# Moving the scores' matmuls next to the values' product in a pipelined macaron kernel on Trainium2

## The chip, the cores and the metric

The kernel runs on one core of one Trainium2 chip. The time is what the device takes for one execution, in microseconds (us); lower is better. The kernel before took 2442.0 us (median of three runs, 2439.76 to 2442.17).

## The reference, cut to what matters

Four sequences of 4096 rows of 512 numbers pass through half of a feed-forward layer, an attention in which each query sees 13 neighbouring keys, and the other half of the feed-forward layer:

```python
x = x + 0.5 * ffn(layernorm(x), ffn_w, ffn_b)     # both operands rounded to a 6-bit grid in blocks of 32
x = x + attention(layernorm(x), qkv_w, qkv_b, rpb, proj_w, proj_b)
x = x + 0.5 * ffn(layernorm(x), ffn_w, ffn_b)
# attention: 16 heads of 32, query i sees keys clip(i - 6, 0, L - 13) .. + 12
attn = softmax(einsum('bhld,bhlkd->bhlk', q, k[nbr]) + rpb[:, bidx])
out  = einsum('bhlk,bhlkd->bhld', attn, v[nbr]) @ proj_w.T + proj_b
```

## The kernel before, in words

**Tiles and items.** The 16384 rows are 128 tiles of 128 rows. Four tiles make a group of 512 rows. The attention of one group for four of the sixteen heads is an item, so there are 128 items as well, and the loop takes one tile and one item a step. An item's queries are cut into blocks of 30 (16 to 18 blocks an item), and a block of queries meets 42 keys.

**Numbers.** Every float32 operand of a large product is held as a high and a low half in 16-bit floats, so one 128 x 512 product is 12 matmuls (`product`, L146 to L154: high by low, low by high, high by high, over four slices of 128).

**Slots.** Nothing schedules this program but the order in which it is written. Each stage is a Python generator (`first_half`, `values`, `project_qk`, `softmax`, `attend`, `project_out`, `second_half`, `quantised_norms`); `begin` (L162) puts it into a slot, `run_slot` (L165) runs the stages of a slot in the order of their rank, and `yield n, rank` sends the rest of a stage n slots on. Seven slots are a step (`STEP`, L559), and L562 says in which slot each stage of item or tile 0 begins. What an engine is handed in this order it does in this order: a waiting instruction holds up all that is behind it on its engine, and on SP's queue of transfers.

**One step on the PE (TensorE).** In the order of the slots: the second feed-forward's product `pmf` and then the item's scores `ps` (slot 0 of the step), the output projection `pmo` (slot 2), the queries' projection `pmqk` and then the values' product `pv` of the item two steps ahead (slot 3), the keys' projection `pmqk` (slot 4), the first feed-forward's product `pmf` (slot 5), the values' projection `pmv` (slot 6). The six products are each 12 matmuls over the whole 128 x 128 array. The scores are 8 small matmuls a block, 32 rows by 32 columns (`num_active_cols=32`, L433), and the values' product is 4 small matmuls a block, 126 rows by 32 columns (L503). Each matmul has a weight load of its own, so with 17 blocks a step is 144 instructions of the six products, 272 of the scores and 136 of the values' product.

**Buffers.** The six products share three PSUM buffers (`ps_m`, L93), so each product needs the result of the third product before it to be read: `pmv` takes the buffer of the queries' `pmqk`, which VectorE (DVE) empties last, in `put_low(0)` (L371 to L375, called at L384). Scores and values' product have one PSUM buffer each.

**An item's way.** `project_qk` (L349): two products, then `put_high` on ScalarE (ACT) and `put_low` on DVE for queries and keys. `softmax` (L417): scores on PE, bias and sum on DVE (L458, L461), the maximum on DVE (L465), its subtraction on GpSimd (POOL, L467), the exponential on ACT (L469), total and reciprocal on DVE (L472 to L474), the scaling on POOL (L476), the high half twice on ACT (L480, L481) and the low half on POOL (L483) into the one tile `p`, and a transposing transfer to `pT` on SP's queue (L485). `attend` (L488): the values' product from `pT` and the stack `vs` of shifted values (loaded from DRAM at L409), then its two halves into `ring` on ACT and DVE (L530, L536).

**Others that share the queues.** `quantised_norms` (L220) makes two tiles' operand `xT` for `pmf` with DVE, POOL and ACT, and sends it through SP (L205), as `first_half` does for `x2`, the operand of `pmv` and `pmqk`.

Of the kernel before, what the change touches and what calls it, by code (L numbers as in the profile page):

```python
# [64 lines left out]
def macaron_kernel(  # L65
# [63 lines left out]
    def bc(t, n):  # L129

        return t.unsqueeze(2).to_broadcast([t.shape[0], t.shape[1], n])
# [14 lines left out]
    def product(pm, lhs, rhs):  # L146

        n = 0
        for a, b in ((0, 1), (1, 0), (0, 0)):
            for c in range(KC):  # L150
                nc.tensor.matmul(  # L151
                    pm, lhs(a, c), rhs(b, c), start=(n == 0), stop=(n == 3 * KC - 1)
                )
                n += 1  # L154
# [7 lines left out]
    def begin(slot, stage, rank=5):  # L162
        slots.setdefault(slot, []).append((rank, stage))
# [155 lines left out]
    def span(j):  # L319

        q0 = min(j * QN, length - QN)
        return q0, min(max(q0 - NS, 0), length - KN)

    def kind(j):
        return 1 if j == 0 else 2 if j == n_blocks - 1 else 0

    def late(j):

        return QR - QN if j == n_blocks - 1 else 0
# [14 lines left out]
    def item_of(m):  # L344

        g, c = divmod(m, KC)
        return g // NG, g % NG, c

    def project_qk(m):  # L349

        b, g, c = item_of(m)
        xg = x2[b * NG + g]
        t = qkp.tile([P, 2, 2, KN + GT], F16, tag="qk", name=f"qk{m}")
        qk[m] = t
        pms = []

        def project(s):
            pm = ps_m.tile([P, GT], F32, tag="mm", name=f"pmqk{s}_{m}")
            pms.append(pm)
            o = (QO, KO)[s] + c * P  # L360
            product(
                pm,
                lambda a, kc: wt[:, a, kc, o : o + P],
                lambda a, kc: xg[:, a, kc].rearrange("p i q -> p (i q)"),
            )

        def put_high(s):
            bias = qk_b[:, s, c : c + 1]
            nc.scalar.activation(t[:, s, 0, KN:], pms[s], AF.Identity, bias=bias)  # L369

        def put_low(s):  # L371
            bias = qk_b[:, s, c : c + 1]
            nc.vector.scalar_tensor_tensor(  # L373
                t[:, s, 1, KN:], pms[s], bias, t[:, s, 0, KN:], ALU.add, ALU.subtract
            )  # L375

        project(0)
        yield 1, 5
        project(1)
        put_high(0)  # L380
        if g > 0:
            nc.scalar.copy(t[:, :, :, :KN], halo[:, c])  # L382
        yield 1, 6
        put_low(0)  # L384
        put_high(1)
        if c == KC - 1:
            del x2[b * NG + g]
        yield 1, 0
        put_low(1)
        yield 2, 8  # L390
        if g + 1 < NG:
            nc.scalar.copy(halo[:, c], t[:, :, :, GT:])
# [24 lines left out]
    def softmax(m):  # L417

        b, g, c = item_of(m)
        j0, j1 = group_blocks[g]  # L420
        n = j1 - j0
        t = qk.pop(m)


        ps = ps_s.tile([P, 3, 2, 256], F32, tag="s", name=f"ps{m}")
        for i in range(n):
            q0, k0 = (KN + at - g * GT for at in span(j0 + i))
            q0 -= late(j0 + i)
            u, w = divmod(i, PSB)
            for part, sides in ((0, 2), (1, 1)):  # L430
                for h in range(4):
                    rows = slice(h * D, (h + 1) * D)
                    nc.tensor.matmul(  # L433
                        ps[rows, u, :sides, w * KN : (w + 1) * KN],
                        t[rows, 0, part, q0 : q0 + QR], t[rows, 1, :sides, k0 : k0 + KN],
                        start=part == 0, stop=part == 1,
                    )

        def pieces(i, e):

            while i < e:
                u, w = divmod(i, PSB)
                whole = max((e - i) // PSB, 1) if w == 0 else 1
                f = min(e, (u + whole) * PSB)
                yield slice(u, u + whole), slice(w, w + (f - i) // whole)
                i = f

        yield 1, 9
        sf = sfp.tile([P, MAXB, KN], F32, tag="sf", name=f"sf{m}")
        s4 = sf.rearrange("p (u w) k -> p u w k", w=PSB)  # L450
        p4 = ps[:, :, :, : PSB * KN].rearrange("p u a (w k) -> p a u w k", k=KN)
        first = 1 if kind(j0) == 1 else 0
        last = n - (1 if kind(j1 - 1) == 2 else 0)
        for i, e in ((0, first), (first, last), (last, n)):
            for u, w in pieces(i, e):
                o = s4[:, u, w, :]
                bias = table[:, kind(j0 + i), c, :].unsqueeze(1).unsqueeze(1).to_broadcast(o.shape)
                nc.vector.tensor_tensor(o, p4[:, 0, u, w, :], bias, ALU.add)  # L458
        for u, w in pieces(0, n):
            o = s4[:, u, w, :]  # L460
            nc.vector.tensor_tensor(o, o, p4[:, 1, u, w, :], ALU.add)  # L461
        yield 1, 2
        s = sf[:, :n, :]
        top = sm.tile([P, MAXB], F32, tag="top", name=f"top{m}")
        nc.vector.tensor_reduce(top[:, :n], s, AX.X, ALU.max)  # L465
        yield 1, 4
        nc.gpsimd.tensor_tensor(s, s, bc(top[:, :n], KN), ALU.subtract)  # L467
        yield 1, 9
        nc.scalar.activation(s, s, AF.Exp, scale=alpha)  # L469
        yield 1, 4  # L470
        total = sm.tile([P, MAXB], F32, tag="total", name=f"total{m}")
        nc.vector.tensor_reduce(total[:, :n], s, AX.X, ALU.add)  # L472
        nc.vector.reciprocal(total[:, :n], total[:, :n])  # L473
        nc.vector.tensor_tensor(total[:, :n], total[:, :n], p_scale[:, :n], ALU.mult)  # L474
        yield 1, 4
        nc.gpsimd.tensor_tensor(s, s, bc(total[:, :n], KN), ALU.mult)  # L476
        yield 2, 8
        p = p_tile
        ph = p[:, :n, :KN]
        nc.scalar.copy(ph, s)  # L480
        nc.scalar.copy(p[:, :n, 2 * KN : KV], ph)  # L481
        yield 2, 4
        nc.gpsimd.tensor_tensor(p[:, :n, KN : 2 * KN], s, ph, ALU.subtract)  # L483
        pT = ptp.tile([P, MAXB, P], F16, tag="pT", name=f"pT{m}")
        nc.sync.dma_start_transpose(out=pT[:, :n, :], in_=p[:, :n, :].rearrange("p n k -> p (n k)"))  # L485
        probs[m] = pT
# [71 lines left out]
    EARLY = 3  # L558
    STEP = 7  # L559

    F1, V, QK, SC, PV, OUT, F2 = 5, 2 * STEP + 6, 5 * STEP + 3, 6 * STEP, 8 * STEP + 3, 13 * STEP + 2, 12

    def add_bias(t, b):
        nc.gpsimd.tensor_tensor(xs[t], xs[t], b, ALU.add)  # L564
# [27 lines left out]
    for t in range(NT):  # L592
        k = t * STEP
# [16 lines left out]
    for m in range(n_items):  # L610
        k = m * STEP
        begin(k + QK, project_qk(m))
        begin(k + SC, softmax(m), 6)
        begin(k + PV, attend(m), 6)
    for n in range(n_batch * NG):
        k = n * GROUP * STEP
# [295 lines left out]
```

## Time and profile before

| what | value |
|---|---|
| runs (us) | 2442.17, 2442.00, 2439.76; median 2442.0 |
| the profiled execution | 2436.42 us, its span 2434.6 us |
| mean granted TensorE clock | 0.992 |
| step (from one item's scores to the next, 1201.9 to 1220.7 us as an example) | 18.80 us: PE 18.07 busy, DVE 16.42, POOL 15.89, ACT 10.41 |
| six products | 380 ns a matmul as the profile models it; a new one starts every 216 ns |
| scores `ps` L433 | 17536 matmuls, 164.0 us and 162.0 us busy in two shapes |
| values' product `pv` L503 | 8768 matmuls, 90.3 us busy |

The profile is one execution. An engine's busy time overlaps itself on PE (a matmul's end is modelled), so starts are compared with starts here. "Idle before" is the time that an engine stood still ahead of an instruction, with what ended it; "issue" means that nothing the profile shows was waited for. A row of the timeline joins instructions of one kind that follow each other: start, length, engine, line, what is written from what, shapes, count.

### The profile page before, as it was taken

What the parts mean: (1) busy time and instruction counts of PE and PEld (TensorE: products, weight loads), DVE (VectorE), ACT (ScalarE), POOL (GpSimd) and SP (SyncE); (2) the same over time, 40 slices, a digit from 0 to 9 for tenths busy, and PEclk for the clock granted to TensorE, in tenths of its full rate; (3) what the DMA queues carried; (4) which work ended last, traced back from release to release, by engine and by line L of the source; (5) the groups of instructions that cost most, each with busy time, mean ns of one, the idle gap of its engine ahead of it and who ended that gap; (6) DMA issues with size and microseconds to landing.
All of it is one profiled execution on the core that took longest, in us unless ns stands there. A gap on an engine that the chain in (4) does not pass through costs nothing.

```text
span 2434.6 us, 82394 instructions
## 1 busy us (share of the span) xinstructions
PE 2295.3 (94%) x35539; PEld 1113.3 (46%) x35539; DVE 2039.3 (84%) x3588; ACT 1321.0 (54%) x2080; POOL 1988.3 (82%) x2012
## 2 busy tenths in 40 slices
PE   0799999999999999999999999999999999999986
PEld 0344444444444444444444444444444444444442
DVE  8788888888888888888888888888888888888776
ACT  4455555555555555555555555555555555555442
POOL 5578888888888888878888888888888888888777
PEclk9899999999999999999999999999999999999998
DMA  5678788787787777778877778777777777777753
GB/s 154 143 145 153 153 161 156 143 152 150 147 159 155 148 147 157 147 144 157 154 146 158 144 152 157 155 148 152 154 140 154 156 157 139 159 148 143 135 110 92
DMA packets 925701, 360.59 MB, mean 148 GB/s; under 512 B 718876, under 2 KB 889752, under 8 KB 925336
## 3 DMA queue, kind: packets, MB, share of 16 engines
q1 hardware_dynamic: 924992, 354.79, 74.4%
q8 instruction: 278, 4.55, 0.8%
q14 instruction: 87, 0.71, 0.1%
q10 hardware_dynamic: 344, 0.53, 0.1%
HBM read 110.15 MB, written 67.29 MB: 73 GB/s over the span
## 4 chain that ended last, share of the span: by engine, by line
PE 67%; DVE 16%; ACT 8%; DMA 5%; issue 3%; POOL 2%; SPq 0%; ACTq 0%; POOLq 0%; DVEq 0%
PE pmf L151 16%; PE pmqk L151 16%; PE pmo L151 13%; PE pmv L151 12%; PE ps L433 6%; DVE total L474 4%; DMA xT<-hlq 4%; DVE total L472 3%; PE pv L503 3%; ACT sf L469 3%; ACT qk L369 2%; DVE qk L373 2%; ACT ring L530 1%; DVE total L473 1%; ACT qk L382 1%
## 5 line engine op out<-in xcount | busy, mean ns | idle before, releaser
L151 PE MATMUL pmf<-wt,xT 128*128 128x512 f16 x3048 | 702.7, 380 | 18.1 <-DMA xT<-hlq 17.7
L151 PE MATMUL pmqk<-x,wt 128*128 128x512 f16 x3072 | 708.6, 380 | 6.0 <-DMA x<-hln 5.3
L151 PEld LDWEIGHTS <-xT 128*128 128x128 f16 x3048 | 296.9, 98 | 386.6 <-DMA xT<-hlq 31.0
L151 PEld LDWEIGHTS <-wt 128*128 128x128 f16 x3072 | 290.2, 98 | 343.3 <-issue 10.2
L246 POOL TENSOR_TENSOR yq<-yq,r 128x1024 f32<-128x1024 f32 (+1 forms) x141 | 246.3, 1747 | 200.5 <-DVE r L244 200.5
L151 PE MATMUL pmv<-wt,x 128*128 128x512 f16 x1536 | 353.5, 380 | 23.5 <-DVE qk L373 14.4
L151 PE MATMUL pmo<-wt,ring 128*128 128x512 f16 x1536 | 356.2, 382 | 2.8 <-issue 2.5
L310 ACT CAST vt<-pmv 128x512 f16<-128x512 f32 x128 | 74.9, 585 | 469.1 <-PE pmv L151 469.1
L564 POOL TENSOR_TENSOR x<-x,half_ffn_b 128x512 f32<-128x512 f32 x256 | 327.3, 1279 | 0.1
L275 DVE SCALAR_TENSOR_TENSOR x<-pmf,coef,x 128x512 f32<-128x512 f32 x256 | 179.7, 702 | 136.9 <-PE pmf L151 136.5
L530 ACT ACTIVATE ring<-pv 128x510 f16<-128x510 f32 (+8 forms) x224 | 82.3, 414 | 368.4 <-PE pv L503 368.4
L180 DVE BATCH_NORM_STATS2 stn<-x 128x6 f32<-128x512 f32 x384 | 265.3, 691 | 9.3 <-DMA x<-in_L_attn_x_dram 0.6
L151 PEld LDWEIGHTS <-x 128*128 128x128 f16 x1536 | 149.9, 98 | 221.6 <-issue 46.4
L251 POOL TENSOR_TENSOR yq<-q,sc 128x1024 f32<-128x1024 fp8e4 (+1 forms) x141 | 246.6, 1749 | 0.0
L249 ACT ACTIVATE q<-yq,nudge 128x1024 fp8e4<-128x1024 f32 (+1 forms) x141 | 150.0, 1064 | 141.6 <-POOL yq L246 133.4
L151 PEld LDWEIGHTS <-ring 128*128 128x128 f16 x1536 | 140.5, 98 | 162.5 <-issue 5.5
L233 ACT ACTIVATE yq<-x,nbq,rsq 128x512 f32<-128x512 f32 x254 | 194.5, 809 | 31.4 <-POOL nbq L192 26.3
L476 POOL TENSOR_TENSOR sf<-sf,total 128x714 f32<-128x714 f32 (+2 forms) x128 | 178.6, 1395 | 37.9 <-DVE total L474 37.4
L483 POOL TENSOR_TENSOR p<-sf,p 128x714 f16<-128x714 f32 (+2 forms) x128 | 192.5, 1504 | 1.2 <-ACT p L480 1.1
L186 POOL TENSOR_SCALAR rsq<-mv 128x2 f32<-128x2 f32 (+1 forms) x141 | 132.0, 936 | 75.0 <-DVE mv L181 72.4
L467 POOL TENSOR_TENSOR sf<-sf,top 128x714 f32<-128x714 f32 (+2 forms) x128 | 180.3, 1409 | 13.8 <-DVE top L465 13.3
L458 DVE TENSOR_TENSOR sf<-ps,table 128x210 f32<-128x210 f32 (+5 forms) x288 | 126.4, 485 | 74.9 <-PE ps L433 74.4
(145 smaller groups left out, 3524.9 us busy)
## 6 DMA issues: line engine op xcount, KB each, us to landing
vs<-vd SPq DMA_DIRECT2D x144, 357.0 KB
x<-in_L_attn_x_dram SPq DMA_DIRECT2D x128, 256.0 KB
vd<-vt SPq DMA_DIRECT2D x128, 256.0 KB
out_dram<-x SPq DMA_DIRECT2D x128, 256.0 KB
vs<-vd SPq DMA_DIRECT2D x24, 378.0 KB
vs<-vd SPq DMA_DIRECT2D x24, 315.0 KB
rows<-in_L_attn_qkv_w_dram SPq DMA_DIRECT2D x12, 256.0 KB
xT<-hlq SPq DMA_TRANSPOSE x141
```

The costliest lines, as they stand in the source:

```text
L151: nc.tensor.matmul(pm, lhs(a, c), rhs(b, c), start=(n == 0), stop=(n == 3 * KC - 1))
L180: nc.vector.bn_stats(st, xs[t])
L233: nc.scalar.activation(y[:, u], xs[t], AF.Identity, bias=nb[:, u : u + 1], scale=rs[:, u : u + 1])
L246: nc.gpsimd.tensor_tensor(yb, yb, bc(r, QB), ALU.mult)
L249: nc.scalar.activation(q8, y, AF.Identity, bias=nudge, saturate=False)
L251: nc.gpsimd.tensor_tensor(yb, q8.rearrange("p u (n q) -> p (u n) q", q=QB), bc(sc, QB), ALU.mult)
L275: nc.vector.scalar_tensor_tensor(xs[t], pm, cf, xs[t], ALU.mult, ALU.add)
L433: nc.tensor.matmul(ps[rows, u, :sides, w * KN : (w + 1) * KN], t[rows, 0, part, q0 : q0 + QR], t[rows, 1, :sides, k0 : k0 + KN], start=par ...
L467: nc.gpsimd.tensor_tensor(s, s, bc(top[:, :n], KN), ALU.subtract)
L476: nc.gpsimd.tensor_tensor(s, s, bc(total[:, :n], KN), ALU.mult)
L483: nc.gpsimd.tensor_tensor(p[:, :n, KN : 2 * KN], s, ph, ALU.subtract)
L564: nc.gpsimd.tensor_tensor(xs[t], xs[t], b, ALU.add)
```

## The change

Scores begin three slots later, in slot 3 of the step and with the highest rank there, so that they stand behind the queries' projection and behind the values' product of the item that is two steps ahead. The values' product of the same item stays in its slot, 14 slots after the scores and not 17. One wait of two slots in `softmax` becomes one of one slot (ahead of L478). `project_qk` comes back with rank -1 and not 6 in the slot after the keys' product, so `put_low(0)` and `put_high(1)` are written first in that slot. No instruction is added or taken out; 22 instructions of PE that only wait on a semaphore are fewer.

```diff
@@ project_qk
         if g > 0:
             nc.scalar.copy(t[:, :, :, :KN], halo[:, c])
-        yield 1, 6
+        yield 1, -1
         put_low(0)
         put_high(1)
@@ softmax
         nc.gpsimd.tensor_tensor(s, s, bc(total[:, :n], KN), ALU.mult)
-        yield 2, 8
+        yield 1, 8
         p = p_tile
@@
-    F1, V, QK, SC, PV, OUT, F2 = 5, 2 * STEP + 6, 5 * STEP + 3, 6 * STEP, 8 * STEP + 3, 13 * STEP + 2, 12
+    F1, V, QK, SC, PV, OUT, F2 = 5, 2 * STEP + 6, 5 * STEP + 3, 6 * STEP + 3, 8 * STEP + 3, 13 * STEP + 2, 12
@@
         begin(k + QK, project_qk(m))
-        begin(k + SC, softmax(m), 6)
+        begin(k + SC, softmax(m), 7)
         begin(k + PV, attend(m), 6)
```

In the built program the order on PE in the middle of the run becomes `pmf, pmo, pmqk, pv, ps, pmqk, pmf, pmv` where it was `pmf, ps, pmo, pmqk, pv, pmqk, pmf, pmv`. On DVE the queries' `put_low` (L373) comes right behind the scores' two additions (L458, L461) and ahead of `ring` (L536), where it stood behind `ring` and the softmax's total (L472 to L474). On ACT the keys' `put_high` (L369) comes ahead of the exponential (L469) and of the norm (L233), and `p` (L480, L481) behind the norms' casts (L200). On POOL one of two bias additions (L564) goes between `p`'s low half (L483) and the maximum's subtraction (L467). On SP's queue the transposes of `xT` and `x2` (L205) come ahead of that of `pT` (L485), where they stood behind it; in every fourth step the six loads of a stack (L409) stand directly ahead of `pT`.

## The prediction

> **What bounds the kernel now.** First the page.
>
> ```profile
> span 2434.6 us, 82394 instructions
> PE 2295.3 (94%) x35539; PEld 1113.3 (46%) x35539; DVE 2039.3 (84%) x3588; ACT 1321.0 (54%) x2080; POOL 1988.3 (82%) x2012
> ...
> q8 instruction: 278, 4.55, 0.8%
> ```
>
> PE is the bound. Keep the last line: a queue of its own brings instructions, 278 packets for PE's 35539 + 35539, so 255.7 in a packet: blocks of 256. Then PE's timeline over a step.
>
> ```profile
> 1201.86 2.75 PE L151 MATMUL pmf<-wt,xT 128*128 128x512 f16 x12
> 1204.54 1.35 PE L433 MATMUL ps<-qk 32*32 32x84 f16 x144
> 1205.82 2.76 PE L151 MATMUL pmo<-wt,ring 128*128 128x512 f16 x12
> 1208.42 2.75 PE L151 MATMUL pmqk<-x,wt 128*128 128x512 f16 x12
> 1211.11 0.79 PE L503 MATMUL pv<-pT,vs 126*32 126x30 f16 x72
> 1211.83 2.76 PE L151 MATMUL pmqk<-x,wt 128*128 128x512 f16 x12
> 1214.43 2.75 PE L151 MATMUL pmf<-wt,xT 128*128 128x512 f16 x12
> 1217.60 2.75 PE L151 MATMUL pmv<-wt,x 128*128 128x512 f16 x12 [0.41 <-DVE qk L373]
> 1220.66 2.55 PE L151 MATMUL pmf<-wt,xT 128*128 128x512 f16 x11 [0.32 <-DMA xT<-hlq]
> ```
>
> From start to start a product takes 2.59 us ahead of another product (1214.43 less 1211.83 is 2.60) and 2.68 to 2.69 ahead of a tiled stretch: entering one costs 0.09. The step has two kinds of stall: `pmv` waits for DVE, `pmf` for a transpose. PE's waits give them, and a third:
>
> ```profile
> PE pmf L151 <- DMA xT<-hlq: 17.7, 18, 5.4
> ...
> PE pmv L151 <- DVE qk L373: 14.4, 60, 1.3
> ...
> PE ps L433 <- issue: 10.1, 8, 2.6
> ```
>
> What is the third? Two of its eight places:
>
> ```profile
> 1039.90 1.26 PE L433 MATMUL ps<-qk 32*32 32x84 f16 x132
> 1043.65 0.20 PE L433 MATMUL ps<-qk 32*32 32x42 f16 x4 [2.49 <-issue]
> ```
>
> ```profile
> 2343.13 1.26 PE L433 MATMUL ps<-qk 32*32 32x84 f16 x133
> 2346.95 0.32 PE L433 MATMUL ps<-qk 32*32 32x42 f16 x11 [2.56 <-issue]
> 2347.21 4.07 PE L151 MATMUL pmo<-wt,ring 128*128 128x512 f16 x12
> ```
>
> PE stops inside a stretch, with nothing to wait for, and goes on 2.5 us later. I numbered PE's instructions in the program's order: all eight stops fall at number 185 of a block of 256, the blocks in which q8 brings them. PE waits for its own instructions. In the second case `pmo` then takes 4.07 us and not 2.76, and the windows view has the granted clock at 0.65 over 2347.0 to 2351.1.
>
> **How that wait works.** A product uses 24 instructions in 2.59 us, a block in 27 us. A tiled stretch is far hungrier: 144 score matmuls with their loads, 288 instructions, go in 1.28 us (1204.54 to 1205.82), and from edge to edge of a block inside a stretch it is 1.05 to 1.07. From q8's packet records I took, for each block, when PE reached it, when the following packet started and ended, and when PE used it. No packet starts before PE nears its block (4.4 us before at the earliest, in a slow product: about 45 instructions that PE reads ahead), it takes 0.9 to 1.5, and its block is never used earlier than 1.24 us after its end; all eight stops sit at 1.3 to 1.7. So the block after next is asked for only when PE enters the next one. For the 137 edges deeper than 64 in a stretch it is 2.9 to 7.2 us (mean 4.6) from reaching the edge to having the next block. **Two edges in one tiled stretch thus stop PE,** unless the first is so near its start that the packet was asked for during the product ahead.
>
> [...]
>
> **The change part by part.** The sum is made on the profiled execution (2436.4 us; 2434.6 span and 1.8 around it), which is 5.6 below the median of the runs; I add the difference to the median.
>
> *One stretch, not two.* Four changes of mode a step (in, out, in, out) become three: the values' product is 126 x 32 and the scores 32 x 32, so the one between them stays, as far as I can tell. 128 x 0.09 = **-12**. No such pair is in the trace of before: 0 if the middle change costs two, -24 if nothing.
>
> *Queries' low part first (L373).* From the end of the scores to `pmv` there are now two products, 5.2 us. DVE has ahead of `pmv`'s release 1.07 (L458) + 0.94 (L461) + 0.74 (L373) = 2.75 us, where it had the ring, the total and its reciprocal, and the scores long past. That stall goes. Start to start it is 93 times over 2.59 + 0.03, 33.6 us together (the waits view's 14.4 counts from a modelled end): **-33**. Next late would be DVE itself: about 16 us of work in 17.5, its last cast ending 0.8 us before the next scores end, with 2.4 more before `pmv` suffers. ACT's `put_high` of the keys now stands ahead of exponential and norm; it waits for the keys' product, 2.6 us after the scores; yq (1.52) then ends at 5.0, DVE's L239 wants it at 5.35. POOL has 15.9 us of work a step; its maximum subtraction can start at 4.2 and its operand is ready at 4.6. Covered, thinly; uncovered, each costs tenths a step, taken as nothing.
>
> *SP's queue.* `xT` and `x2` pass `pT`. `pmf`'s wait for `xT` (1209.61: `pT` occupied the queue 6.48 us ahead of it) goes: **-8** in the steady part, start to start. `pT` pays: before, it landed 26 to 33 us after the scores began and was used at 42.5. Now it is used two steps less a values' product later, 34.2, and lands one slot (2.6) sooner, 23.5 to 30; behind the six stack loads (last landed 8 to 10 us after their first issue) the margin falls to about 1 us in one step of four. Taken as nothing; 1 us more would be 32.
>
> *Head and tail.* The last scores move behind a product and a values' product (3.3 us), and the end already waits 7.3 us for `pT`: **+3** (0 to +7).
>
> *The stretch itself.* Its instructions were 272 and 136 for 17 blocks; joined they are 408, of which 152/256 = 59% of the positions hold two edges. Counted in both programs' orders: before, 15 of 128 score stretches hold two edges, all with the first under 48 in (three full stops, ten none); **after, 76 of 128, of which the first edge is at 48 or more in 51, at 16 to 47 in 15, below in 10**; 9 more have the second edge just behind the stretch. A full stop: 2.5 us in the trace, up to 4.6 - 1.07 - 0.2 (read ahead) = 3.3 from the mean turnaround; I take 2.7, as most of those edges lie in the values' product, near the transposes. 51 x 2.7 = 138; 15 x 1.4 (half) = 21; 10 x 0.7 (the 15 of before lost 9.5) = 7; 9 x 1.0 (0.6 to 2.1 in before) = 9; less before's 22: **+153**, between +110 (2.2 for a full stop) and +199 (3.3).
>
> *Clock.* Stretch and stop together last some 4.5 us; of three full stops in before one halved the clock for 1.3 us. 14 x 1.3 = **+18** (0 to +45).
>
> Sum: -12 - 33 - 8 + 3 + 153 + 18 = +121: profiled 2557, median 2442 + 121 = **2563 us**.
>
> **Rivals.**
> - *The fetch stays hidden* (not slower). Place: the second edge in the joined stretch. If a block were asked for one block earlier, only -12 - 33 - 8 + 3 = -50 remains: 2392. For it: 112 of 128 steps never show the stop. Against: their stretches have no two edges, or the first in reach of the read-ahead. It decides from a turnaround of about 2.2 us (1.07 + 0.2 + a stop of 0.9, which 76 times, less before's 22, eats the 50); the shortest of 137 is 2.9. Chance 0.11.
> - *Exposed, but at the quick end:* packets start 0.9 us after the edge, full stop 2.2, clock untouched: -12 - 33 - 8 + 3 + 110 = +60, 2502. Chance 0.22.
> - *Exposed, slow, and the clock drops often* [...]: +199 + 45 - 50 = +194, 2636. Chance 0.20.
> - *A new wait for `pT`* behind the stack loads, 1 us in 32 steps, on top of the forecast: about 2595. For it: the margin. Against: each stop gives the transposes time. Chance 0.05, inside the slow cases.
>
> Forecast 0.42.
>
> **How the numbers follow.** The range takes in the two exposed rivals and the bounds of mode change and tail: 2480 (quick stops, a free middle change) to 2645; outside lie the hidden fetch and a little beyond both ends, some 0.18. 0.2% (5 us) is about what this measurement can tell from no change. Faster: the hidden fetch, 0.11. Same: a quick fetch that just balances the gain, 0.02. Slower: 0.87.
>
> **What would show it.** Right: PE's `pv` and `ps` with "issue" waits of 150 to 220 us in all, at numbers of one residue of 256; rows of some `ps`, then a gap of 2 to 3.5 us, then the rest; q8 still 278 packets. The `pmv` wait for L373 gone, `pmf` hardly waiting for `xT`. From `pv`'s start to `ps`'s start 0.60 to 0.67 us where there is no stop tells the middle change. Wrong: joined stretches of 408 instructions without stops; or PE waiting for `pT`, DVE or PSUM instead.

## The result, and the profile after

| | before | after |
|---|---|---|
| median of 6 runs each, same chip (us) | 2442.09 (2437.24 to 2444.04) | 2640.28 (2633.34 to 2657.50) |
| ratio of after to before | | 1.0826, 95% interval 1.079 to 1.0863 |
| profiled execution: span (us) | 2434.6 | 2638.6 |
| mean granted TensorE clock | 0.992 | 0.958 |
| PE's stops inside the tiled stretches (a gap over 0.25 us between two starts) | 9, 12.3 us | 61, 162 us |

The change costs 198 us; the forecast was +121. First the page of the kernel after: span, busy time of the engines, the granted clock in tenths over 40 slices, and the queue that brings PE its instructions.

```profile
span 2638.6 us, 82283 instructions
PE 2365.6 (90%) x35539; PEld 1158.5 (44%) x35539; DVE 2030.3 (77%) x3588; ACT 1325.1 (50%) x2080; POOL 1987.2 (75%) x2012
...
PEclk9899999999899999999999999999999999989998
...
q8 instruction: 278, 4.55, 0.7%
```

Two things can be read here. PE does the same 35539 matmuls and its share of the span falls from 94% to 90%: it stands still more. And its busy time grows all the same, from 2295.3 to 2365.6: some of the same matmuls have become slower, by 70 us. q8 brings the same 278 packets and 4.55 MB; what is fetched has not changed, only that PE takes more of it in one stretch (for 17 blocks 408 instructions, where it took 272 and 136).

PE's waits after the change (us in total, times, longest):

```profile
PE ps L433 <- issue: 150.6, 61, 4.6
...
PE pv L503 <- DMA pT<-p: 20.3, 4, 11.7
...
PE pmqk L151 <- issue: 12.9, 6, 3.3
PE pmf L151 <- DMA xT<-hlq: 10.6, 5, 5.4
```

The row of `pmv` waiting for L373 is gone, `xT` is nearly gone, and "issue" in the scores has gone from 10.1 us in 8 to 150.6 in 61. Two steps of PE's timeline show it, the first without a stop, the second with one:

```profile
1148.83 0.69 PE L503 MATMUL pv<-pT,vs 126*32 126x30 f16 x68
1149.45 1.42 PE L433 MATMUL ps<-qk 32*32 32x84 f16 x136
1150.80 2.76 PE L151 MATMUL pmqk<-x,wt 128*128 128x512 f16 x12
```

```profile
1188.90 0.69 PE L503 MATMUL pv<-pT,vs 126*32 126x30 f16 x68
1189.53 1.20 PE L433 MATMUL ps<-qk 32*32 32x84 f16 x111
1193.20 0.51 PE L433 MATMUL ps<-qk 32*32 32x42 f16 x25 [2.47 <-issue]
1193.64 3.98 PE L151 MATMUL pmqk<-x,wt 128*128 128x512 f16 x12
1197.46 2.75 PE L151 MATMUL pmf<-wt,xT 128*128 128x512 f16 x12
```

Both stretches are 68 + 136 small matmuls. In PE's instructions numbered in the program's order, the first edge of a block of 256 lies 186 into the first stretch, so the second is outside. It lies 105 into the second stretch, and the second edge at 361; PE stops after 68 + 111 = 179 matmuls and their loads, that is after 358 instructions and a few that only wait. So this is the stop of the forecast, at the place of the forecast. Then comes what the forecast had too small: the `pmqk` behind it takes 3.98 us and not 2.76. The windows view (length; PE, PEld, DVE, ACT and POOL busy; then the granted clock) has it at 0.72 there, and at 1.00 behind a stop of nearly the same length a hundred us later:

```profile
1293.53 0.29 PE L433 MATMUL ps<-qk 32*32 32x84 f16 x14 [2.52 <-issue]
1293.76 2.76 PE L151 MATMUL pmqk<-x,wt 128*128 128x512 f16 x12
```

```profile
1193.30:1198.30 5.00, 5.00 (x41) 2.11 (x40) 3.90 (x7) 0.64 (x2) 2.16 (x3) 0.72 0.98 197
1293.50:1298.00 4.50, 4.47 (x34) 2.15 (x35) 4.08 (x8) 1.44 (x3) 1.57 (x2) 1.00 1.27 169
```

**Where the 204 us between the two spans are.** Taken from the records of both traces, start to start:

| part | us |
|---|---|
| stops inside the tiled stretches, 162 against 12.3 | +150 |
| gaps for instructions inside products, behind a stretch included, 23.6 against 11.2 | +12 |
| clock: products with starts 427 ns apart instead of 216, 81.6 against 11.4; and the rest of the scores behind a stop at a lower rate, 3 | +73 |
| pauses of about 0.1 us inside the scores, 115 against 2 | +13 |
| `pmf` to `pmv` (the wait for L373), 367.4 to 339.7 | -28 |
| `pmv` to `pmf` (the wait for `xT`), 317.5 to 310.9 | -7 |
| the changes of mode: a product ahead of a tiled stretch or of another product, 2.683 to 2.590 us, 119 times | -11 |
| `pv` waiting for `pT`, most of it at the end, 20.3 against 13.0 | +7 |
| sum | +209 |

The parts together are 5 us more than the difference of the spans; where they overlap is open. The row of the short pauses can be seen in the step without a stop above: 136 score matmuls fill 1.35 us up to the next product there (1149.45 to 1150.80), where 144 filled 1.28 before (1204.54 to 1205.82). The pauses sit near the 70th score matmul, most of them 0.6 to 0.7 us behind the last matmul of `pv`, at no fixed instruction number. So they come with the new place of the scores and are not waits for a block of instructions; what they wait for is open.

### The profile page after: what moved, and what is told of

It reads as the page before. It is cut to its first block, busy times and chain, and to the rows that moved or that the text cites. A ratio compares the mean times of both kernels' runs of the same rounds, so it can differ in the third digit from the quotient of the medians.

```text
span 2638.6 us, 82283 instructions
## 1 busy us (share of the span) xinstructions
PE 2365.6 (90%) x35539; PEld 1158.5 (44%) x35539; DVE 2030.3 (77%) x3588; ACT 1325.1 (50%) x2080; POOL 1987.2 (75%) x2012
## 3 DMA queue, kind: packets, MB, share of 16 engines
q8 instruction: 278, 4.55, 0.7%
## 4 chain that ended last, share of the span: by engine, by line
PE 84%; issue 7%; DVE 4%; DMA 2%; POOL 2%; ACT 1%; SPq 0%; DVEq 0%; POOLq 0%; ACTq 0%
PE pmqk L151 27%; PE pmf L151 23%; PE pmv L151 12%; PE pmo L151 12%; PE ps L433 7%; PE pv L503 3%; DMA pT<-p 1%; POOL x L564 0%; DVE hlq L204 0%; POOL yq L251 0%; POOL yq L246 0%; DMA x<-hln 0%; DVE fw L749 0%; DVE sc L239 0%; DVE stn L180 0%
## 5 line engine op out<-in xcount | busy, mean ns | idle before, releaser
L151 PE MATMUL pmqk<-x,wt 128*128 128x512 f16 x3072 | 781.0, 408 | 14.6 <-issue 12.9
L151 PEld LDWEIGHTS <-wt 128*128 128x128 f16 x3072 | 306.5, 103 | 407.9 <-issue 109.3
L369 ACT ACTIVATE qk<-pmqk,qk_b 128x512 f16<-128x512 f32 x256 | 176.1, 688 | 559.1 <-PE pmqk L151 558.1
L458 DVE TENSOR_TENSOR sf<-ps,table 128x210 f32<-128x210 f32 (+5 forms) x288 | 126.3, 484 | 311.9 <-PE ps L433 311.9
L467 POOL TENSOR_TENSOR sf<-sf,top 128x714 f32<-128x714 f32 (+2 forms) x128 | 179.1, 1399 | 205.9 <-DVE top L465 202.9
L433 PE MATMUL ps<-qk 32*32 32x84 f16 (+1 forms) x17536 | 195.3, 190 | 150.6 <-issue 150.6
L564 POOL TENSOR_TENSOR x<-x,half_ffn_b 128x512 f32<-128x512 f32 x256 | 327.1, 1278 | 0.1
L433 PEld LDWEIGHTS <-qk 32*32 32x32 f16 x17536 | 168.2, 90 | 166.9 <-issue 157.9
L373 DVE SCALAR_TENSOR_TENSOR qk<-pmqk,qk_b,qk 128x512 f16<-128x512 f32 x256 | 190.5, 744 | 60.4 <-ACT qk L369 60.4
L151 PEld LDWEIGHTS <-x 128*128 128x128 f16 x1536 | 150.6, 98 | 188.8 <-DMA x<-hln 5.6
L151 PEld LDWEIGHTS <-ring 128*128 128x128 f16 x1536 | 150.0, 98 | 180.9 <-ACT ring L530 0.3
L200 ACT CAST hlq<-yq 128x1024 f16<-128x1024 f32 (+1 forms) x141 | 135.3, 959 | 157.2 <-POOL yq L251 157.2
L233 ACT ACTIVATE yq<-x,nbq,rsq 128x512 f32<-128x512 f32 x254 | 193.0, 803 | 14.7 <-POOL nbq L192 14.7
L483 POOL TENSOR_TENSOR p<-sf,p 128x714 f16<-128x714 f32 (+2 forms) x128 | 191.8, 1499 | 2.1 <-ACT p L480 2.1
```

Of the source, the lines that this page charges most:

```text
L151: nc.tensor.matmul(pm, lhs(a, c), rhs(b, c), start=(n == 0), stop=(n == 3 * KC - 1))
L200: nc.scalar.copy(hl[:, :, 0, :], y)
L233: nc.scalar.activation(y[:, u], xs[t], AF.Identity, bias=nb[:, u : u + 1], scale=rs[:, u : u + 1])
L373: nc.vector.scalar_tensor_tensor(t[:, s, 1, KN:], pms[s], bias, t[:, s, 0, KN:], ALU.add, ALU.subtract)
L433: nc.tensor.matmul(ps[rows, u, :sides, w * KN : (w + 1) * KN], t[rows, 0, part, q0 : q0 + QR], t[rows, 1, :sides, k0 : k0 + KN], start=par ...
```

## The experiments

The theory: a stretch of tiled matmuls that holds two edges of a block of 256 instructions stops PE for the fetch, and the stop drags the clock down. Rivals: the loss comes from something else in the new order (transposes, ACT's or DVE's new order, a change of mode), or from the small edits in the queues. Where a time of before is needed, each experiment has its own runs of it on its own chip; the ratio is to those.

**1. The rank alone.** Kernel before with

```diff
-        yield 1, 6
+        yield 1, -1
```

in `project_qk`, nothing else.

> The order of before, with the queries' low part first alone (rank -1). If pmv's wait for it was DVE's order and nothing else, its 33.6 us go and nothing comes instead: 2409 (2403 to 2418), the issue waits inside the scores' stretches as in before (8, some 10 us). Rival: what is now behind it on DVE (ring, total) is late in its turn and the wait moves to pv, pmo or the transposes: 2435 to 2445.

Measured: 2411.11 (2401.86 to 2416.63), ratio 0.987 (0.9845 to 0.9895). As expected: the part of the change that gains does so by itself, without moving the scores. The wait for L373, 14.4 us in 60 in before, is gone from its profile. What stood ahead of L373 can be read in the step of before that the prediction shows:

```profile
1212.55 0.70 ACT L369 ACTIVATE qk<-pmqk,qk_b 128x512 f16<-128x512 f32 x1
```

```profile
1214.33 0.94 DVE L472 TENSOR_REDUCE total<-sf 128x18 f32<-128x756 f32 x1 [0.35 <-ACT sf L469]
1215.31 0.27 DVE L473 RECIPROCAL total<-total 128x18 f32<-128x18 f32 x1
1215.61 1.28 DVE L474 TENSOR_TENSOR total<-total,p_scale 128x18 f32<-128x18 f32 x1
1216.81 1.40 DVE L373 SCALAR_TENSOR_TENSOR qk<-pmqk,qk_b,qk 128x512 f16<-128x512 f32 x2
```

The queries' high half is done at 1213.25, and L373 starts at 1216.81, behind L472, which stood still for 0.35 us until the exponential ended.

**2 and 3. The stretch shortened in both orders.** Kernel before and kernel after with the scores' second pass left out:

```diff
-            for part, sides in ((0, 2), (1, 1)):
+            for part, sides in ((0, 2),):
...
-                        start=part == 0, stop=part == 1,
+                        start=True, stop=True,
```

> Before without the second pass of the scores (the low half of the queries is left out of the scores), as the partner of the next run. 68 score matmuls fewer a step at 8.3 ns are 0.57 us, 73 in all, and score stretches of 136 instructions cannot hold two edges of a block, so before's 22 us of stops go too: 2347 (2335 to 2370; pmv's wait for DVE may take some back). No issue wait in ps.

> The changed kernel without the second pass of the scores (the low half of the queries is left out of the scores): the joined stretch has 272 instructions and not 408, two edges in 9 steps and not in 76, all in reach of the read-ahead. PE waiting for its own instructions: the stops nearly vanish (under 25 us), the clock stays up, and the change is a gain as it was meant to be: 2315 (2295 to 2335), 20 to 45 below its partner. Rival, that values' product and scores side by side hurt each other (array, PSUM, mode change): about half or all of the 198 stays, 2440 to 2550.

Measured: before shortened 2379.22 (2377.19 to 2381.04), ratio 0.9744 (0.9716 to 0.9772); after shortened 2338.74 (2334.44 to 2339.43), ratio 0.9572 (0.9548 to 0.9596). The pair is what counts: with a joined stretch of 272 instructions, in which 9 steps hold two edges (76 in after), **the same move that costs 198 us gains 40**. The waits for instructions in the scores shrink to this:

```profile
PE pv L503 <- DMA pT<-p: 21.9, 5, 12.7
...
PE ps L433 <- issue: 7.0, 2, 4.0
```

The rival of the order's other effects falls: they are all still there. Two stops are left, 7.4 us from start to start, in stretches with the first edge under 48; that all of them lay in reach of the read-ahead was too much said. Both absolute times were missed, shortened after by 24 us. Shortened before is 32 us above its forecast for two reasons. In the starts its score stretches are 71 us shorter (172.8 to 102.0 us together), where 95 were reckoned for the matmuls and the stops. And PE, now quicker, arrives earlier at the transposes:

```profile
PE pmf L151 <- DMA xT<-hlq: 29.7, 24, 5.4
...
PE pmv L151 <- DVE qk L373: 12.3, 30, 1.8
```

(In the starts, the intervals `pmv` to `pmf` take 16 us more than in before and `pmf` to `pmv` 6 less, 10 us more together.) So taking work from PE in the old order is worth less than its length: 71 us less of scores made the span 59 us shorter.

**4. The stretch lengthened in the old order.** Kernel before, the first pass made twice:

```diff
-            for part, sides in ((0, 2), (1, 1)):
+            for n_, (part, sides) in enumerate(((0, 2), (0, 2), (1, 1))):
...
-                        start=part == 0, stop=part == 1,
+                        start=n_ < 2, stop=n_ != 1,
```

> The order of before, with the first pass of the scores made twice (same result), so that the scores' stretch alone has 408 instructions, as the joined one had; nothing is moved. Counted in its order: two edges in 74 steps, the first at 48 or more in 55. PE waiting for its own instructions: 73 for the added matmuls, 55 x 2.75 + 13 x 1 + 14 x 1.5 less 22 = +163 of stops, some +75 of clock, pmv's wait mostly gone (-30): 2720 (2670 to 2770), with issue waits in ps of some 180 us. Rival, that the neighbourhood of values' product and scores did it: 2515, with issue waits as in before.

Measured: 2797.23 (2789.18 to 2803.64), ratio 1.1451 (1.1419 to 1.1484). The scores alone are now 408 instructions, `pv` is elsewhere, nothing is moved, and the stops are there:

```profile
PE ps L433 <- issue: 178.5, 64, 5.6
...
PE pmo L151 <- issue: 25.9, 13, 5.3
```

The rival (2515, the added matmuls alone) falls. The size was missed by 77: 71 stops of 199 us together, 187 more than in before where 163 were reckoned; gaps at the start of `pmo` behind the stretch, which I had not counted; and 89.5 us of products at half rate (11.4 in before). How the miss divides over the last two I have not worked out.

**5. The same stretches, other instruction numbers.** Kernel after, with the product into `pmb` at the start made six times, which puts 120 instructions ahead of everything:

```diff
-            product(pmb, lambda s, c: vbx[:, s, c, :], lambda s, c: wt[:, s, c, PO : PO + dim])
+            for _ in range(6):
+                product(
+                    pmb, lambda s, c: vbx[:, s, c, :], lambda s, c: wt[:, s, c, PO : PO + dim]
+                )
```

> The changed kernel with one product early in the run (pmb) made six times over, the same result each time: 120 instructions more ahead of everything, so that all later instructions lie elsewhere in their blocks. Counted in its order, two edges with the first at 48 or more fall into 57 of the joined stretches, and only one of these is among the 51 of the changed kernel. PE waiting for its own instructions: the stops move to the 57 counted items (long stops in under 5 of the 51 old ones), the time is 2640 + 13 for the products + some 20 for more edges: 2670 (2645 to 2700). Rival, that stops belong to certain items, buffers or transfers: they stay with their items, 2653.

Measured: 2660.85 (2656.44 to 2665.27), ratio 1.0909 (1.0884 to 1.0935). The total hardly tells; which steps stop tells all. Counted in the program's order, 51 items of the kernel after hold two edges with the first 48 or more instructions into the stretch, in the shifted kernel 57 items do, and the two sets share one item. A stop over 1.7 us is in 56 items of after, among them **all 51 of its own set** and 2 of the other set; in the shifted kernel in 63 items, among them **all 57 of its own** and 3 of the other. Item 64, first in after and then in the shifted kernel, from the values' product on:

```profile
1347.92 0.79 PE L503 MATMUL pv<-pT,vs 126*32 126x30 f16 x72
1348.64 1.31 PE L433 MATMUL ps<-qk 32*32 32x84 f16 x128
```

```profile
1361.68 0.81 PE L503 MATMUL pv<-pT,vs 126*32 126x30 f16 x72
1362.42 1.07 PE L433 MATMUL ps<-qk 32*32 32x84 f16 x100
1365.38 0.54 PE L433 MATMUL ps<-qk 32*32 32x42 f16 x28 [1.89 <-issue]
```

The data, the transfers and the order are the same; only the numbering differs, and the stop comes and goes with it. A cause that belongs to an item (its loads, its transposes, its size) is ruled out.

**6. A product between the two.** Scores one slot later than in the change, behind the keys' `pmqk`, with the two small edits of the change:

```diff
-    F1, V, QK, SC, PV, OUT, F2 = 5, 2 * STEP + 6, 5 * STEP + 3, 6 * STEP, 8 * STEP + 3, 13 * STEP + 2, 12
+    F1, V, QK, SC, PV, OUT, F2 = 5, 2 * STEP + 6, 5 * STEP + 3, 6 * STEP + 4, 8 * STEP + 3, 13 * STEP + 2, 12
```

> The changed kernel with the scores one slot later still, behind the keys' projection: values' product, one product (24 instructions, 2.59), scores. Two edges in one stretch in 11 steps, but in about half the steps one edge in the values' product and the next in the scores, some 3.5 apart where the turnaround is 4.2 in the mean. PE waiting for its own instructions: short stops, 0.7 in some 45 steps and little in the rest, 40 to 60 in all, no clock to speak of, the waits for DVE and xT gone, four changes of mode as before: 2430 (2405 to 2460). Rival, that scores right after the keys' product or in this half of the step wait for something else: over 2500 with another name at PE's wait.

Measured: 2477.01 (2466.09 to 2482.32), ratio 1.015 (1.0126 to 1.0174): 163 below the change, but 47 above the forecast.

```profile
PE ps L433 <- issue: 44.0, 25, 2.6
PE pv L503 <- DMA pT<-p: 38.5, 22, 8.0
```

The stops had been reckoned at 40 to 60 us and are 48.6, in 25 places instead of some 45, so one product in between shortens them (median 2.05 us; 2.59 in after) and doesn't take them away. What was not foreseen is the second row: the scores start so late that `pT`'s margin is used up, `pmqk` to `pv` being 26.9 us over its length in 20 steps. The clock adds about 9 (24.2 against 15.4 with the rank alone). That is 36 of the 47. Of the other 11, some 7 are short pauses inside the scores (69 of about 0.1 us), as in after; 4 I have not placed.

**7. The move alone.** Kernel after with the old rank back (`yield 1, 6`).

> The changed kernel with project_qk's rank back at 6: the queries' low part comes behind ring and maximum on DVE, 4.5 after the scores' end where pmv wants its buffer at 5.2. If the rank is without weight once the scores are moved: 2640 (2625 to 2660), no wait of pmv for L373. Rival, that it is what keeps pmv free: 2655 to 2680 with that wait back.

Measured: 2628.09 (2619.2 to 2636.99), ratio 1.0775 (1.074 to 1.081). Its stops are there, and `pmv` hardly waits for L373 any more:

```profile
PE ps L433 <- issue: 148.8, 62, 5.1
...
PE pmv L151 <- DVE qk L373: 1.0, 2, 0.7
```

In before that wait was 14.4 us in 60. Once the scores stand elsewhere, it all but ends whichever rank `project_qk` has. The saving of experiment 1 is thus not the rank's alone; rank and move each bring it, and not twice.

**8. An attempt to go on from experiment 1.** Rank -1, and the transposes of `xT` and `x2` let past that of `pT` by one slot:

```diff
-        yield 2, 4
+        yield 3, 4
```

> The order of before, with the queries' low part first and the transpose of pT one slot later (yield 3 for yield 2), so that xT and x2 pass it on SP's queue; the scores stay where they were. pmf's waits for xT in the steps (11 with the queries first) go and pT, with 11 to 14 to spare, hides the slot: 2400 (2390 to 2412), 10 below the queries first alone. Rival, that the transposes only change places and pT or the tile p is late: 2411 or more.

Measured: 2423.92 (2420.47 to 2427.2), ratio 0.994 (0.9926 to 0.9954). The forecast was wrong. The wait for `xT` goes from 16.6 to 8.6 us as meant, but more is lost elsewhere. In the starts, `pmqk` to `pv` takes 12.5 us more than in experiment 1 and `pv` to `pmqk` 10.7 more, and PE waits for instructions in both:

```profile
PE pv L503 <- issue: 14.2, 15, 2.0
PE pmqk L151 <- issue: 10.8, 6, 3.6
```

The stretches hold 18 stops of 21.0 us, where experiment 1 has 12 of 14.0. In the steps with one edge in the scores and the next in the values' product, the packet ends more than 4 us after the first edge in 20 of 65, and in 11 of 59 in experiment 1. So packets do come later; that a transpose beside them is the cause is a guess, which no run here tests.

**9. The change without its move.** Both small edits (rank -1, and `yield 1, 8`), scores where they were.

> The changed kernel less its main part: the scores stay behind the second feed-forward's product, and the two small edits are made (queries' low part first, one slot less ahead of p). Two edges in one stretch in 9 steps, all but one under 16. If the third edit is without weight here, as the time of the queries first alone: 2411 (2400 to 2425); the whole loss of the change is then the place of the scores. Rival, that an earlier pT collides with the loads ahead of xT: 2425 to 2445, with pmf waiting longer for xT.

Measured: 2408.19 (2406.69 to 2409.75), ratio 0.9873 (0.9856 to 0.9889). This beats both kernels and can't be told from experiment 1. From here, moving the scores behind `pv` takes the time to 2640: the whole loss, 232 us, is the place of the scores.

**The clock, counted over all traces.** This is read from all eleven traces. I took every record of a halved clock. In after, the 49 records, all at 0.5, begin on a grid of 3413.33 ns, within 2 ns, from the first to the last; the other traces show the same grid within 2 ns. A window is here one step of that grid. Ahead of the slow `pmo` of before, PE stood still for 2.56 us, less than a window. I reckoned for each window of the grid the share in which PE was at work (a product's matmul 0.21 us, a small one up to the next start). In the middle of the eleven runs (20 us after the first small matmul to 60 us before the last, windows already at half clock left out), 156 of 194 drops follow a window with a share below 0.415, and of 6831 windows without a drop only 4 are below it. Between 0.415 and 0.52 both occur, 38 drops and 59 windows without one; above 0.52 there is no drop. The bound was drawn on these same windows. So **2.0 us of standing still within one window of 3.41 was enough in 156 of 160**, and somewhat less was in 38 of 97. By an estimate from these two lengths, a stop of L between 2.0 and 4.0 us meets the 2.0 in (L - 0.59)/3.41 of its possible places on the grid. Counted over all idle stretches of PE, of whatever cause:

| PE idle for (us) | cases | followed by a drop | share by the formula |
|---|---|---|---|
| 1.0 to 1.5 | 67 | 0 | 0 |
| 1.5 to 1.8 | 34 | 1 | 0 |
| 1.8 to 2.0 | 32 | 14 | 0 |
| 2.0 to 2.2 | 62 | 27 | 0.44 |
| 2.2 to 2.5 | 61 | 32 | 0.51 |
| 2.5 to 3.0 | 78 | 52 | 0.62 |
| 3.0 to 3.5 | 23 | 18 | 0.78 |
| over 3.5 | 48 | 48 | 0.85 to 1 |

The row at 1.8 to 2.0 shows that the bound is not sharp for the stop alone; a window holds smaller gaps too. The grid also accounts for the pair of windows above: of the stop of 2.47 us, 2.2 us of standing still lie in one window, and that of 2.52 is split into 0.9 and 1.8. About a quarter of the drops last two windows or more, 50 of 197. Which ones, the traces show too: those in which PE stands still in the first slow window as well. With under 0.5 us of gaps there, none of 143 drops lasts longer than one window; from 0.5 to 0.75 us, 2 of 6; above, all 48. What stays open: no experiment changed the length of a stop alone.

## Why the prediction was right, and which term was too small

**The cause was right.** "Two edges in one tiled stretch thus stop PE" was taken from eight stops in the trace of before, and experiments 2 to 5 leave no other cause for the stops: they go from 61 to 2 when few stretches hold two edges, come in the old order when the stretch is long enough, and follow the numbering. The packets of q8 say the same: the 60 stops over 1 us in after end 1.19 to 2.03 us behind the end of a packet, 1.40 in the median. (A few packets are longer than the 0.9 to 1.5 us of the prediction; the longest in before took 3.8.) The rivals of a hidden fetch and of the quick end fall with 162 us of stops.

**The stops: forecast +153, measured +150 inside the stretches and +12 behind them and in products.** The forecast took off 22 us for before; 12.3 of before's stops lie inside stretches. By class: the 46 joined stretches with the first edge at 48 or more whose gap could be read from the records all stopped, 2.77 us each (forecast 2.7; by items all 51 of 51). At 16 to 47, 8 of 14 stopped, 15.2 us in all (forecast 21). Below 16, 1 of 9, 1.2 us (forecast 7). Second edge just behind, 3.1 us (forecast 9), with another 12 in gaps inside the products. The turnaround from edge to usable block, for edges deeper than 64, is 4.2 us on average after the change and 4.6 before, and a block is again not used sooner than 1.19 us after its packet's end. One sum was off: the lower bound of +110 does not follow from its terms, as 51 x 2.2 with the others as stated gives +127, or +119 with the smaller classes at their lowest. Nothing rests on it.

**The clock: forecast +18, measured about +73.** This is the term that failed in size: "of three full stops in before one halved the clock for 1.3 us. 14 x 1.3". Both factors were too small. One in three came from three cases; the formula above gives (2.77 - 0.59)/3.41 = 0.64 for the mean full stop, and 40 of the 61 stops (0.66) are followed by a slow product. And the cost of a drop was read from one `pmo` that was partly in the dropped window; a whole window at half rate (a product's matmul every 427 ns and not every 216) costs 3.41 / 2 = 1.7 us, and twice that where it lasts two. Some 44 drops in the middle of the run, 11 of them double, come to 55 x 1.7 = 94 at most, since PE also stands still in part of the slow windows; measured, without before's taken off, are 85. The stated bound of +45 was too low as well. The time, 77 us above the forecast, stayed within the range because the rival of the frequent drops was part of it. That this rival's 2636 lies so near the measured 2640 is luck: it had +199 for the stops and +45 for the clock, the latter the author's estimate, where +150 and +73 were measured.

**The small terms.** `pmv`'s wait: forecast -33, measured -28. `xT`: -8, and -7. Modes: -12, and -11, but the short pauses beside it (+13), which no term had, take it back; `pv` to `ps` is 0.624 us in the middle of a stretch after the change, and before it `pv` to the next product was 0.627, so between 126 x 32 and 32 x 32 nothing of the 0.09 was saved, as taken. Tail and `pT`: +3, measured +7. DVE, ACT and POOL were taken as covered, and the rows of PE's waits that name DVE anew are two single waits, 3.0 us together.

**What was not told apart, without harm:** the -33 stands under the queries' low part, beside the new distance from the scores to `pmv`. Experiments 1 and 7 show that rank and move each bring it alone.

## What to carry to other kernels

Number the instructions of PE and ask, for each stretch of small matmuls, how many blocks of 256 it spans: here a joined stretch with two edges, the first 48 or more instructions in, stopped PE for 2.8 us, while the same matmuls in two stretches, kept apart by two long products, stopped it in 9 places for 12 us in all. A saved change of mode was 0.09 us here (2.683 to 2.590), and the 61 stops in the longer stretches cost 2.7 each on average. And count such a stop at its own length plus about 1.2 us for the clock (an estimate: 73 us over 61 stops here), not at its length alone.

## What the runs showed of the hardware that was not expected

- In all eleven traces the records of a halved clock begin on a grid of 3413.33 ns, which holds through the whole run. Of 160 windows of this grid in which PE was at work for a share of less than 0.415, 156 were followed by half the clock. Where PE stood still for over 0.75 us in the first slow window as well, the half clock lasted beyond it in 48 of 48 drops; with under 0.5 us, in none of 143.
- Where the first of two edges lies 48 or more instructions into a stretch, the numbering alone tells that PE stops: of 51 and 57 items picked by counting in the program, all 51 and all 57 stopped, and 120 instructions more at the start of the program swapped one set for the other.
- One product of 24 instructions between two tiled stretches shortens the stop (experiment 6: 25 stops, median 2.05 us) but doesn't always end it; a product lasts 2.59 us, a block takes 4.2 to 4.6 on average to come.
